# Mirroring half of a band's pixels, and shortening and reordering its reads, in a convolution and involution kernel

## The chip, the cores and the metric

The kernel runs on one core of a Trainium2 chip. The metric is the device time of one execution in microseconds (us); lower is better. Engines are named as in the profile: PE is the matrix engine (PEld its weight loads), DVE is VectorE, ACT is ScalarE, POOL is GpSimd and SP is SyncE. SP and POOL issue the transfers (DMAs); SP through the hardware queue, q1 in the profile, and POOL through the software queue, q0.

## The reference, cut to what matters

Two layers work on `x` of shape 32 x 256 x 32 x 32 (images, channels, rows, columns). Each normalizes its input in groups of eight channels (`_gn`) and adds its result to `x`.

```
# layer 0: 3x3 convolution, 256 to 256 channels, inputs and result quantized to a 10-bit mantissa
x = x + conv3x3(gn(x), weight) + bias
# layer 1: an involution; every pixel has a 7x7 kernel of its own for each of 16 groups of 16 channels
y   = relu(bn(einsum('oc,bchw->bohw', w1, gn(x))))               # 256 to 64 channels
w   = einsum('oc,bchw->bohw', w2, y) + b2                        # 16 groups x 49 taps for each pixel
out[b,g,c,h,w] = sum over k of w[b,g,k,h,w] * patches[b,g,c,k,h,w]   # 7x7 patches of gn(x), padded by 3
x = x + out
```

## The kernel before, in words

The images go through one after the other, in a software pipeline written out by hand (`manual_schedule`): the main loop counts slots n, 16 for each image, and in every slot each piece of work is issued for the image and the part that are due. Within one engine, instructions run in exactly that order; the transfers of a queue are issued in that order too.

**The front of an image** (`front`, a generator that advances one stage in each slot) computes sums for the first normalization (line 213, ACT), the quantized input `xq` (272, ACT), the 3x3 convolution `pc` (326, PE), clips it on DVE (340) and adds it to the image (342). It then normalizes again into `xn` (272), multiplies by w1 into `py` (374, PE), applies the ReLU into `y` (381, ACT) and transposes `xn` by PE (389) into `pixels` (393, ACT), in which a pixel is a partition and channels lie along the free axis.

**The pixels of an image** are cut into K = 4 bands of TR = 8 rows, and each band into two SIDES of JC = 16 columns, so that one side of one band has 8 x 16 = 128 pixels, one for each partition. Partition 16r + j holds row r and column j of the side: column j of the image on the left, column 16 + j on the right.

**The kernels of the involution** come from `weights` (404, PE, into `pw`). `evict` (428, DVE) adds the bias and writes them into a ring `w_sb` with 32 rows of the image. `scatter` (469) sends them from there to a scratch `wd` in device memory, by 28 DMAs for each image, all issued by SP. In `wd` each pixel has a record of WPIX = 1128 numbers (4512 B): seven slots of WB = 160 numbers (640 B), one for each of the seven columns that it contributes to, and 8 numbers of padding. Columns outside of the image have a place as well (S = 38 columns in all).

**A band** is a matrix that holds, for each of the 128 pixels of a side (the contraction), what it contributes to each of the 22 columns around that side. The buffer has 128 partitions, two sides and 22 slots and the padding (3528 numbers) for each side, and there are NBAND = 3 of them, zeroed once. `load_bands` (482) fills one by 16 DMAs, one for each column j of the side. Each takes 8 partitions (`j::16`), for both sides the whole record of 1128 numbers, and places it at slot j, since pixel j reaches slots j to j + 6. What it reads from `wd`, and who issues it:

```
j = i // 2 + i % 2 * JC // 2                          # 0, 8, 1, 9, 2, 10, ...
ap=[[ROW - V, TR], [JC * WPIX, SIDES], [1, WPIX]]
queue = nc.sync if i % SHARE == SHARE - 1 else nc.gpsimd
```

So SP issues columns 11 and 15 and POOL the other 14. `sums` (507, PE) multiplies `pixels` by 19 of the 22 slots of the band into `acc`: on the left slots 3 to 21, on the right 0 to 18, which are the columns inside the image. A first matmul of a band waits until all its 16 DMAs have landed. `add_windows` (523, DVE) adds `acc` to the image, and `store` (528, SP) writes it out; SP also loads the images (105).

In the order of the loop, weights run 18 slots ahead of the sums of their image, the scatter of a band comes one and two slots after the last weights that it needs, and the reads of band k are issued 9 slots ahead of its sums. POOL's instruction stream consists of almost nothing but these reads. Every read on POOL waits for the landing of POOL's eighth read before it, since there are eight semaphores to go round. The first read of a band also waits for the band's scatters and for the sums that used the buffer before. A scatter waits for the reads that last used its rows of `wd`.

Of the kernel before, what the change touches and what calls it, by code (L numbers as in the profile page):

```python
# [10 lines left out]
AF = mybir.ActivationFunctionType  # L11
# [3 lines left out]
B, C, H, W = 32, 256, 32, 32  # L15
# [5 lines left out]
K1, PAD1 = 7, 3  # L21
# [18 lines left out]
TR = RG * XR  # L40
SIDES = 2
JC = W // SIDES
# [3 lines left out]
WINC = JC + K1 - 1  # L46
# [5 lines left out]
V = 2  # L52
A = G // V
WB = G * WIN
PAD = V * (TR - XR)
WPIX = K1 * WB + PAD
# [6 lines left out]
ROW = S * WPIX  # L63
WR = 4
NBAND = 3
SHARE = 8
NPIX = 6
RING = 32
SCRATCH = 4096
# [8 lines left out]
def tile_quant_conv_then_involution(  # L78
# [10 lines left out]
    nc = tc.nc  # L89
# [50 lines left out]
    y_sb = [const.tile([P, N // 2], F32, name=f"y_{i}") for i in range(2)]  # L140
# [9 lines left out]
    wd = dram.tile([H, S, WPIX], F32, name="wd")  # L150
# [22 lines left out]
    bn_scale = const.tile([P, 1], F32, name="bn_scale")  # L173
    nc.vector.tensor_mul(bn_scale, bn[:, 0:1], bn_r)
    bn_shift = const.tile([P, 1], F32, name="bn_shift")
# [4 lines left out]
    for col, cols, at, n in (  # L180
# [4 lines left out]
        to = bass.AP(  # L185
            tensor=wd.tensor,
            offset=wd.offset + col * WPIX + at,
            ap=[[ROW, H], [WPIX, cols], [1, n]],
        )
# [83 lines left out]

    LATER = 1

    CONV = (9, 0, 9, 0)

    def front(b):
# [4 lines left out]
        def stages(n):  # L283
            for _ in range(n):
                yield

        gn = GroupNorm(b, 0)
# [18 lines left out]
        gn = GroupNorm(b, 1)  # L306
        gn.begin(N // NT)
        units = [(nt, mh) for nt in range(N // NT) for mh in range(CH)]
        for s in range(4 * len(units) + 2):
            u, i = divmod(s, 4)  # L310
            if u < len(units):
# [4 lines left out]
                elif i == 0:  # L316
                    pc = ps_c.tile([P, NT], F32, tag="pc", name="pc")
                for n in range(sum(CONV[:i]), sum(CONV[: i + 1])):


                    k = n if n < K0 * K0 else CH * K0 * K0 - 1 - n
                    kh, k = n // (K0 * K0), (k + K0 * K0 // 2) % (K0 * K0)
# [11 lines left out]
            u, i = divmod(s - 3, 4)  # L334
# [25 lines left out]
        for h in range(CH):  # L360
            yield
            to = xn[:, h].rearrange("p (k d r j) -> p d k r j", d=SIDES, r=TR, j=JC)
            at = xt[:, h].rearrange("p (k r d j) -> p d k r j", d=SIDES, r=TR, j=JC)
            gn.apply(h, [(to[:, d], at[:, d]) for d in range(SIDES)])
        yield from stages(2)

        py = ps_m.tile([P, NT], F32, tag="m", name="py")
        for r0 in range(0, H, WR):
            cols = slice(r0 // 2 * W, (r0 + WR) // 2 * W)
            for kh in range(CH):  # L370
                px = xn[:, kh].rearrange("p (k d r j) -> p k r d j", d=SIDES, r=TR, j=JC)[:, r0 // TR]
                for i in range(2):
                    r = r0 % TR + 2 * i
# [4 lines left out]
                        start=kh == 0,  # L378
                        stop=kh == CH - 1,
                    )  # L380
        nc.scalar.activation(y_sb[b % 2], py, AF.Relu, bias=bn_shift, scale=bn_scale)
        yield from stages(5)

        for m in range(0, M, 2):
# [7 lines left out]
            to = pixels[(b * M + m) // 2 % NPIX].rearrange("p i a (v c) -> p (i a) v c", c=GC)  # L392
# [78 lines left out]
    def load_bands(b, k):  # L471

        band = bands[(b * K + k) % NBAND]
        for i in range(JC):
            j = i // 2 + i % 2 * JC // 2
            src = bass.AP(
                tensor=wd.tensor,
                offset=wd.offset + k * TR * ROW + (j + PAD1) * WPIX,
                ap=[[ROW - V, TR], [JC * WPIX, SIDES], [1, WPIX]],
            )  # L480
            queue = nc.sync if i % SHARE == SHARE - 1 else nc.gpsimd
            queue.dma_start(band[j::JC, :, j * WB : j * WB + WPIX], src)  # L482

    def windows(b, m):

# [48 lines left out]
    def due(n, lag):  # L534

        b, i = divmod(n - lag, per)
        return (b, i) if 0 <= b < B else (None, None)

    with tc.manual_schedule():
        fronts = {}  # L540
        for n in range(FRONT, B * per + 2):
            b, i = due(n, FRONT)
            if i == 0:
                fronts[b] = front(b)
# [10 lines left out]
            b, i = due(n, 0)  # L555
            if b is not None and i % 2 == 0:
                sums(b, i // 2)
            b, i = due(n, 1)
# [6 lines left out]
            b, i = due(n, 2)  # L565
            if b is not None and i == 2 * (M - 1 - SIDES):
                store(b, 0)
            b, i = due(n, -LEAD)
# [3 lines left out]
            for part in range(2):  # L572
                b, i = due(n, -LEAD + 1 + part)
# [4 lines left out]
            b, i = due(n, LOAD)  # L578
# [3 lines left out]
            b, i = due(n, 3 - 4 * NBAND)  # L582
            if b is not None and i % 4 == 0:
                load_bands(b, i // 4)
# [38 lines left out]
```

## Time and profile before

| | |
|---|---|
| Time, median of 3 runs | 1371.49 us (1369.76 to 1373.4) |
| The profiled execution: its time, and its span | 1367.45 us, 1365.7 us |
| PE, busy | 1262.2 us (92%) |
| POOL, busy (all but 34 us issuing band reads) | 1012.0 us (74%) |
| DVE, ACT, busy | 819.5 us (60%), 725.7 us (53%) |
| Bytes moved by DMA | 369.95 MB, mean 271 GB/s |
| Band reads on POOL | 1792 of 70.5 KB, 548 ns each to issue, 4.8 us to land |
| Band reads on SP | 256 of 70.5 KB |
| Scatters on SP | 896 of 160 KB |

The profile shows one execution. An engine's busy time is the union of its instructions; the line number names the source line. A queue's share is the time that its packets took, as a part of the span of all 16 DMA engines. A line of waits names the engine that idled, what it was about to do, and what it waited for, then the total in us, how often, and the longest. "issue" stands where the profile shows nothing that was waited for.

### The profile page before, as it was taken

Reading aid. Unit: us, or ns where it says so; the run is one execution under the profiler, and the core shown is the slowest. Engines: PE = TensorE matmul, PEld = TensorE weight load, DVE = VectorE, ACT = ScalarE, POOL = GpSimd, SP = SyncE. Lnnn points to the kernel's source line nnn. Section 1 sums busy time; section 2 is a strip of 40 time slices with the busy share of each in tenths; the row PEclk is TensorE's granted clock in tenths of the full one; section 3 lists DMA queues with packets and bytes.
Section 4 is the critical chain, followed back from the end, with each engine's and each line's share of the span. In section 5 each row is a group of like instructions: output and inputs, shape, how many; then the busy total and the mean of one; then the engine's idle time right before and its main releaser. Section 6 shows DMA issues by size and latency. Waiting matters only on the chain.

```text
span 1365.7 us, 69351 instructions
## 1 busy us (share of the span) xinstructions
PE 1262.2 (92%) x29440; PEld 808.8 (59%) x29440; DVE 819.5 (60%) x2539; ACT 725.7 (53%) x1699; POOL 1012.0 (74%) x1818
## 2 busy tenths in 40 slices
PE   4999999999999999999999999999999998999675
PEld 2456556666566656665665666656666665666553
DVE  3466566566666656665756666666666565666542
ACT  6765656455555546565545565545656554653300
POOL 9067777777777777777777877777777777777786
PEclk9999999999999999999999999999999999999987
DMA  6199999999999999999999999999999999999996
GB/s 224 25 245 286 271 279 287 287 281 278 287 287 285 285 296 276 289 280 270 288 287 283 276 272 280 292 293 288 278 293 276 262 286 290 267 291 274 273 272 194
DMA packets 364834, 369.95 MB, mean 271 GB/s; under 512 B 77104, under 2 KB 306800, under 8 KB 364272
## 3 DMA queue, kind: packets, MB, share of 16 engines
q1 hardware_dynamic: 278512, 235.93, 57.9%
q0 software_dynamic: 86016, 129.60, 34.3%
q8 instruction: 234, 3.83, 1.2%
q14 instruction: 72, 0.59, 0.1%
HBM read 184.46 MB, written 180.76 MB: 267 GB/s over the span
## 4 chain that ended last, share of the span: by engine, by line
PE 67%; DMA 19%; issue 4%; POOL 4%; ACT 3%; DVE 2%; SPq 1%; POOLq 0%; DVEq 0%; ACTq 0%
PE pc L326 27%; PE acc L507 21%; DMA band<-wd 14%; PE pw L404 12%; DMA wd<-w_sb 5%; POOL band L482 4%; PE py L374 3%; PE pt L389 3%; ACT junk L213 1%; DVE w_sb L428 1%; SPq L469 1%; ACT xn L272 0%; DMA x<-in_x 0%; SPq L482 0%; ACT xq L272 0%
## 5 line engine op out<-in xcount | busy, mean ns | idle before, releaser
L482 POOL DMA_DIRECT2D band<-wd x1792 | 978.0, 548 | 342.9 <-DMA band<-wd 224.0
L428 DVE TENSOR_TENSOR w_sb<-pw,late_sb 128x224 f32<-128x224 f32 (+7 forms) x1280 | 331.0, 324 | 437.7 <-PE pw L404 437.6
L326 PE MATMUL pc<-xq,wq 128*128 128x496 f16 (+3 forms) x2304 | 536.0, 379 | 24.7 <-ACT xq L272 18.6
L507 PE MATMUL acc<-band,pixels 64*32 64x190 f32 (+1 forms) x16384 | 429.7, 331 | 52.0 <-DMA band<-wd 34.8
L326 PEld LDWEIGHTS <-wq 128*128 128x128 f16 x2304 | 206.5, 98 | 319.0 <-issue 106.4
L507 PEld LDWEIGHTS acc<-band,pixels 64*32 64x32 f32 x16384 | 303.2, 107 | 142.3 <-issue 94.9
L404 PE MATMUL pw<-late_sb,y 64*32 64x224 f32 (+1 forms) x8192 | 288.0, 331 | 18.7 <-issue 17.8
L523 DVE TENSOR_TENSOR x<-acc,x 128x380 f32<-128x380 f32 (+1 forms) x512 | 262.7, 513 | 31.6 <-PE acc L507 22.7
L404 PEld LDWEIGHTS pw<-late_sb,y 64*32 64x32 f32 x8192 | 186.2, 106 | 46.7 <-issue 31.9
L393 ACT COPY pixels<-pt 128x512 f32<-128x512 f32 x128 | 73.7, 576 | 241.9 <-PE pt L389 241.9
L213 ACT ACTIVATE junk<-x 128x512 f16<-128x512 f32 (+1 forms) x192 | 146.3, 762 | 14.4 <-DVE x L342 11.9
L213 ACT ACTIVATE junk<-x,mean 128x1024 f16<-128x1024 f32 x128 | 147.1, 1149 | 4.3
L244 ACT ACTIVATE s<-back,eps 128x2 f32<-128x2 f32 x64 | 18.9, 296 | 199.1 <-DVE back L229 199.0
L340 DVE TENSOR_SCALAR q<-pc 128x512 f16<-128x512 f32 x128 | 87.3, 682 | 17.1 <-PE pc L326 17.1
L272 ACT ACTIVATE xn<-x,off,rstd 128x512 f32<-128x512 f32 x128 | 96.2, 800 | 0.0
L342 DVE SCALAR_TENSOR_TENSOR x<-q,early_sb,x 128x512 f32<-128x512 f16 x128 | 94.8, 740 | 0.3
L389 PEld LDWEIGHTS pt<-ident,xn 128*128 128x128 f32 x512 | 63.8, 142 | 26.5 <-issue 3.6
L389 PE MATMUL pt<-ident,xn 128*128 128x128 f32 x512 | 77.7, 275 | 0.1
L272 ACT ACTIVATE xq<-x,off,rstd 128x1024 f16<-128x1024 f32 x64 | 75.8, 1227 | 0.2 <-PE pc L326 0.2
L374 PEld LDWEIGHTS py<-xn,early_sb 128*64 128x64 f32 x2048 | 62.6, 138 | 17.0 <-ACT mean L234 8.1
L374 PE MATMUL py<-xn,early_sb 128*64 128x64 f32 x2048 | 67.5, 224 | 3.1 <-ACT xn L272 2.2
L234 ACT ACTIVATE mean<-back 128x2 f32<-128x2 f32 x64 | 12.5, 196 | 101.4 <-DVE back L229 101.4
(40 smaller groups left out, 372.6 us busy)
## 6 DMA issues: line engine op xcount, KB each, us to landing
wd<-w_sb SPq DMA_DIRECT2D x896, 160.0 KB
band<-wd POOLq DMA_DIRECT2D x1792, 70.5 KB, 4.8
x<-in_x SPq DMA_DIRECT2D x64, 512.0 KB
out<-x SPq DMA_DIRECT2D x64, 512.0 KB
band<-wd SPq DMA_DIRECT2D x256, 70.5 KB
band<-in_w SPq DMA_DIRECT2D x2, 1152.0 KB
late_sb<-in_late SPq DMA_DIRECT2D x1, 616.0 KB
wd<-band SPq DMA_DIRECT2D x2, 180.0 KB
```

Of the source, the lines that this page charges most:

```text
L213: nc.scalar.activation(junk[:, n0:n1], src[:, h, n0:n1], func, bias=bias, accum_out=self.sums[:, i : i + 1])
L272: nc.scalar.activation(dst, src, AF.Identity, bias=self.off[:, one], scale=self.rstd[:, one])
L326: nc.tensor.matmul(pc.rearrange("p (r c) -> p r c", c=W)[:, r0 - nt * RT : r1 - nt * RT, c0:c1], wq[:, kh, k, mh * P : (mh + 1) * P], xq[: ...
L340: nc.vector.tensor_scalar(q, pc, F16_MAX, -F16_MAX, ALU.min, ALU.max)
L342: nc.vector.scalar_tensor_tensor(xt[:, mh, cols], q, bias_sb[:, mh : mh + 1], xt[:, mh, cols], ALU.add, ALU.add)
L374: nc.tensor.matmul(py[i * CR : (i + 1) * CR, cols], w1_sb[:, kh, :], px[:, r : r + 2], start=kh == 0, stop=kh == CH - 1,)
L389: nc.tensor.transpose(pt[:, i, h * P : (h + 1) * P], xn[:, h, (m + i) * P : (m + i + 1) * P], ident)
L404: nc.tensor.matmul(pws[i][t * TW : (t + 1) * TW, : dj.stop - dj.start, r], y_sb[b % 2][half, (r0 // 2 + r) * W : (r0 // 2 + r + 1) * W], w ...
L428: nc.vector.tensor_tensor(to, of[:, :, d0:d1], bias[:, :, d0:d1], ALU.add)
L482: queue.dma_start(band[j::JC, :, j * WB : j * WB + WPIX], src)
L507: nc.tensor.matmul(at[t * TW : (t + 1) * TW, h, :, f - top : l - top], px[p, a, v * GC : v * GC + TW], of[:, :, a, f - top : l - top, v], ...
L523: nc.vector.tensor_tensor(x_at, of, x_at, ALU.add)
```

## The change

The right side of each band is mirrored in the partitions: partition 16r + j now holds column 31 - j of the image on the right, and still column j on the left. `xn` is written in that order (the source is read backwards along the columns), so `pixels` follow; `y`, which has to keep the columns' natural order, is undone by a second ReLU instruction for the right side, that reads `py` backwards.

With this, the pixels of one DMA lie equally far from the two edges of the image. The slots of columns outside of the image are left out of the read: `cut` of the seven slots, 3 for j = 0, 2 for j = 1 and 1 for j = 2, on both sides. The reads of j = 0 and 1, which are the two shortest, are issued by SP (`BY_SYNC`), the other 14 by POOL. The columns are taken in another order (`ORDER`), one from each quarter of the 16 in turn. For j = 15 the two columns (15 and 16) are neighbours in `wd` and in the band, and the read becomes one run of 2256 numbers in each of 8 partitions. The number of DMAs and their places in the loop stay.

```diff
-SHARE = 8
+BY_SYNC = (0, 1)
+ORDER = (0, 4, 8, 12, 2, 5, 9, 13, 3, 1, 6, 10, 14, 7, 11, 15)
...
+    def backwards(at):
+
+        step, n = at.ap[-1]
+        return bass.AP(tensor=at.tensor, offset=at.offset + step * (n - 1), ap=[*at.ap[:-1], [-step, n]])
...
-            gn.apply(h, [(to[:, d], at[:, d]) for d in range(SIDES)])
+            gn.apply(h, [(to[:, 0], at[:, 0]), (to[:, 1], backwards(at[:, 1]))])
...
-        nc.scalar.activation(y_sb[b % 2], py, AF.Relu, bias=bn_shift, scale=bn_scale)
+        to = y_sb[b % 2].rearrange("p (r d j) -> p d r j", d=SIDES, j=JC)
+        of = py.rearrange("p (r d j) -> p d r j", d=SIDES, j=JC)
+        for d in range(SIDES):
+            at = of[:, d]
+            nc.scalar.activation(to[:, d], backwards(at) if d else at, AF.Relu, bias=bn_shift, scale=bn_scale)
...
-        for i in range(JC):
-            j = i // 2 + i % 2 * JC // 2
+        side = WINC * WB + PAD
+        for i, j in enumerate(ORDER):
+            cut = max(0, PAD1 - j)
+            n = (K1 - cut) * WB + PAD
             src = bass.AP(
                 tensor=wd.tensor,
-                offset=wd.offset + k * TR * ROW + (j + PAD1) * WPIX,
-                ap=[[ROW - V, TR], [JC * WPIX, SIDES], [1, WPIX]],
+                offset=wd.offset + k * TR * ROW + (j + PAD1) * WPIX + cut * WB,
+                ap=[[ROW - V, TR], [(W - 1 - 2 * j) * WPIX - cut * WB, SIDES], [1, n]],
             )
-            queue = nc.sync if i % SHARE == SHARE - 1 else nc.gpsimd
-            queue.dma_start(band[j::JC, :, j * WB : j * WB + WPIX], src)
+            to = band[j::JC]
+            to = bass.AP(
+                tensor=to.tensor,
+                offset=to.offset + (j + cut) * WB,
+                ap=[to.ap[0], [side + (JC - 1 - 2 * j - cut) * WB, SIDES], [1, n]],
+            )
+            queue = nc.sync if j in BY_SYNC else nc.gpsimd
+            queue.dma_start(to, src)
```

## The prediction

> **What bounds the kernel now.** I read the page first: busy times, then the DMA queues.
>
> ```profile
> span 1365.7 us, 69351 instructions
> ...
> PE 1262.2 (92%) x29440; PEld 808.8 (59%) x29440; DVE 819.5 (60%) x2539; ACT 725.7 (53%) x1699; POOL 1012.0 (74%) x1818
> ...
> DMA  6199999999999999999999999999999999999996
> ...
> q1 hardware_dynamic: 278512, 235.93, 57.9%
> q0 software_dynamic: 86016, 129.60, 34.3%
> q8 instruction: 234, 3.83, 1.2%
> ```
>
> Two resources look full: PE (92%), and the DMA engines, whose packets fill 57.9 + 34.3 + 1.3 = 93.5% of sixteen engines' span. VectorE and ScalarE have over a third of the span free. To separate the two I cut the trace where py's matmuls start, once per image. From 49.9 to 1283.3 us there are 31 intervals, mean 39.8 us, shortest 38.3 us. Stage windows (start and end, then the length, busy time by engine, granted clock, DMA share, GB/s):
>
> ```profile
> 642.60:682.30 39.70, 38.91 (x921) 25.03 (x920) 25.31 (x80) 22.55 (x54) 30.10 (x57) 1.00 1.00 285
> 723.30:764.50 41.20, 39.21 (x921) 24.95 (x920) 25.26 (x80) 22.56 (x54) 30.62 (x57) 1.00 0.97 278
> 87.00:1283.00 1196.00, 1147.66 (x27274) 738.29 (x27272) 748.11 (x2326) 660.28 (x1548) 904.64 (x1658) 1.00 0.98 282
> 1283.00:1366.00 83.00, 49.95 (x1534) 38.84 (x1520) 31.90 (x90) 3.12 (x5) 61.11 (x112) 0.82 0.84 244
> ```
>
> A slow image has the same PE work and more PE idle. In the steady stretch PE idles 1196.0 - 1147.7 = 48.3 us: 1.6 us per image is all that faster transfers can return there. In the tail it idles 33 us of 83. What ends the idle time, from the waits (total, times, longest):
>
> ```profile
> POOL band L482 <- DMA band<-wd: 224.0, 285, 2.8
> POOL band L482 <- DMA wd<-w_sb: 55.6, 28, 37.1
> PE acc L507 <- DMA band<-wd: 34.8, 17, 5.1
> PE pw L404 <- issue: 17.8, 17, 1.8
> PE acc L507 <- issue: 15.2, 19, 2.2
> POOL band L482 <- PE acc L507: 0.5, 1, 0.5
> ```
>
> POOL waits for a band buffer to be freed by PE once in the whole run; it waits 285 times for its own earlier transfers, because the order of its instructions makes each wait for the one eight before it. POOL is thus busy or held by DMA for 1355 us. Its last issue for a band comes 7.1 us on average before PE's first use, and landing takes 4.8 us: a margin near 2 us. So PE and the transfers run at almost the same pace, PE could go slightly faster, and late transfers cause part of its pauses. By place, the steady 48.3 us are 25.1 us ahead of acc (band late) and 23.3 us inside pw and conv, mostly with no releaser.
>
> The tail's chain names the transfers:
>
> ```profile
> by line: DMA band<-wd 39.1%; POOL band L482 21.2%; PE acc L507 15.0%; issue 6.7%; PE pw L404 5.1%; DMA wd<-w_sb 3.2%; DVE w_sb L428 2.3%; DVE x L523 1.0%; PE pt L389 1.0%; SPq L469 0.8%; POOLq L482 0.2%
> ```
>
> [...] a 4512 B row on q0 has a median of 182 ns (24.8 GB/s), a mean of 242, and a tenth over 404. [...] instructions come in 16 KiB blocks over a DMA queue. q8 has 234 such packets, mean 1083 ns; PE's pauses without releaser may be these, unproven.
>
> **The change, part by part.**
>
> *Shorter reads.* Columns 0, 1, 2 lose 3, 2, 1 slots of 640 B; with the right half mirrored, the same transfer loses them on columns 31, 30, 29. Eight rows, two sides: 16 x 6 x 640 = 61,440 B per band of 1,155,072, so 5.3% of the band reads and 7.9 MB of 370 (2.1%). Priced by bytes: 61,440 / 4512 = 13.6 rows x 242 ns / 16 engines = 0.21 us per band, 0.82 us per image as a mean over the engines (0.62 at the median row).
>
> *Who reads them.* SP's two reads shrink from 2 x 72,192 to 16 x (2592 + 3232) = 93,184 B. [...] POOL's column 2 saves 9.1 rows x 242 / 16 = 0.14. [...] POOL still issues 14 reads per band at 548 ns and SP two: the comparison of the two programs' orders shows the same counts, the same lanes to wait for, and SP's two still side by side behind the same scatters. No wait is added.
>
> *By quarters.* [...] The stretch to play for is 242 - 182 = 60 ns on 56 rows per engine and image = 3.4 us. [...] I bound it by a quarter of the stretch either way, +-0.84 us per image, and take zero[...].
>
> *Column 15* merges into 8 rows of 9024 B, where column 16 lies beside it. Nearest row: q1's 9216 B packets take 347 ns, against 2 x 182. Four per image, gain 0.07 us or none; POOL's issue could be cheaper than 548 ns, or dearer if it goes by bytes. I take the same.
>
> *ScalarE.* y becomes two instructions of 256 elements: 622 ns for 512 and 1042 for 1024 give 0.82 ns per element, so 768 becomes about 1116, +0.35 us per image. Reading xn backwards has no row; between free and double its element time, up to +0.84 us per image. pw reads y two slots of the loop (near 5 us) later, py comes two stages after xn; ScalarE is free 47%. Without that cover it would be 1.2 x 32 = 38 us. I take zero.
>
> *Sum.* [...] Of the 25.1 us ahead of acc I take two thirds (17 us): on average the relief covers these 0.8 us per image, but they come in bursts of up to 3.9 us; of the 23.3 us elsewhere a quarter (6 us). In the tail, 114 POOL reads go at 0.62 us each (71 us; 62 at bare issue): 3.7% of 71 is 2.6, and 2 us from starting ahead, so 5. Together 28 us: 1367.5 - 28 = 1339.5 for the profiled execution, which is 4 under the median; on the median's footing **1343.5 us**.
>
> **The rivals.** *No change:* PE is the real bound and its pauses are fetch and evictions; for it, PE's 96% in the steady stretch; against it, 34.8 us of waits on bands and POOL's never waiting for PE. Time 1371.
>
> *Larger gain:* all idle on the steady stretch goes and the tail falls to bare issue: 48 + 9 = 57, so 1315. Against it: DMA is not the only cause.
>
> *Slower:* [...] The relief is 1.47 us over 56 rows = 26 ns a row: from a mean row of 268 ns on, transfers are slower than now. [...] about +60 us: 1430; half of that excess gives about 1390. [...]
>
> *Not what it says:* that the slots are still read elsewhere. The changed program's reads are 8x2x648, 808 and 968, so this has no weight.
>
> **The numbers.** Likeliest, 1343.5, with the larger gain beside it: 0.75. No change: 0.12 (within 0.3%, about what a measurement of this kernel can tell from none). Slower: 0.13. The range reaches from near the larger gain's end to just above no change: 1318 to 1376.
>
> **What would show it.** q0 and q1 move 362 MB together with the rest; q1's share falls by more than q0's; the mean 4512 B row stays near 242 ns; intervals between py's starts come to 39.0 us; PE's waits on bands halve. ScalarE gains 32 instructions and no PE wait on y. Wrong if the row's mean passes 268 ns, if PE's idle stays at 48 us while DMA share drops, or if new waits of pw on y appear.

## The result, and the profile after

The changed kernel takes 1351.88 us (median of 20 runs, 1344.72 to 1365.11), the kernel before 1372.43 us (20 runs, 1361.98 to 1386.47). The ratio is 0.9852, with a 95% interval of 0.9831 to 0.9872: 20 us or 1.5% faster. A single run of either kernel can lie 10 us off its median. The profiled execution of the changed kernel took 1362.92 us and is one of its slowest, that of before took 1367.45 us and is one of its faster ones. So I read a second profile of the same kernel beside it, which took 1339.36 us (experiment e11).

The pages' lines on busy times, transfers and queues; first the changed kernel:

```profile
span 1361.1 us, 69383 instructions
...
PE 1264.5 (93%) x29440; PEld 808.0 (59%) x29440; DVE 819.7 (60%) x2539; ACT 733.2 (54%) x1731; POOL 1014.4 (75%) x1818
...
q1 hardware_dynamic: 278512, 229.38, 56.2%
q0 software_dynamic: 81920, 128.28, 33.4%
```

and the same kernel again (e11):

```profile
span 1337.6 us, 69383 instructions
...
PE 1249.6 (93%) x29440; PEld 801.8 (60%) x29440; DVE 820.7 (61%) x2539; ACT 733.2 (55%) x1731; POOL 1014.4 (76%) x1818
```

The bytes are the 7.9 MB fewer that were worked out (6.55 on q1, 1.32 on q0), ScalarE has its 32 instructions more, and the shares of both queues are down. PE's entry differs: the same 29,440 matmuls are "busy" for 1264.5 us in one execution and 1249.6 us in the other. The mean granted clock was 0.980 in the first and 0.990 in the second; busy time times clock gives 1239 and 1238, so here the difference goes with the clock.

By stage, in e11: up to the start of the last py, and after it (start and end, length, busy time by engine, clock, DMA share, GB/s).

```profile
87.00:1255.60 1168.60, 1138.71 (x27278) 734.45 (x27275) 748.91 (x2329) 667.80 (x1580) 909.59 (x1663) 1.00 0.96 283
1255.60:1337.60 82.00, 47.07 (x1526) 36.03 (x1520) 31.90 (x90) 3.36 (x6) 58.65 (x108) 0.84 0.80 235
```

Cut in the same places, the kernel before:

```profile
87.00:1283.30 1196.30, 1147.96 (x27277) 738.31 (x27274) 748.11 (x2326) 660.28 (x1548) 904.88 (x1659) 1.00 0.98 282
1283.30:1365.70 82.40, 49.65 (x1526) 38.82 (x1520) 31.90 (x90) 3.12 (x5) 60.87 (x112) 0.82 0.84 244
```

and the first profile of the changed kernel, cut within 0.3 us of the start of its last py:

```profile
87.00:1277.00 1190.00, 1148.45 (x27276) 739.20 (x27275) 749.15 (x2328) 667.31 (x1579) 909.78 (x1664) 0.99 0.95 277
1277.00:1361.00 84.00, 51.62 (x1535) 37.33 (x1520) 31.90 (x90) 3.73 (x7) 58.14 (x107) 0.79 0.79 233
```

In both the gain lies in the steady stretch, and the tail is as long as it was. Between the kernel before and e11 the stretch shrinks by 1196.3 - 1168.6 = 27.7 us, in the slower profile by some 6 us; the medians, 20 us apart, lie between. PE's idle time there falls from 48.3 to 29.9 us in e11 and to 41.6 us in the other. Between starts of py there are now 38.9 us on average (39.6 in the slower profile), against 39.8.

The waits of the changed kernel (its first profile; totals, times, longest):

```profile
POOL band L500 <- DMA band<-wd: 186.8, 238, 3.6
POOL band L500 <- DMA wd<-w_sb: 86.8, 44, 37.3
PE pw L414 <- issue: 23.7, 21, 2.6
PE acc L525 <- DMA band<-wd: 18.2, 11, 5.3
PE acc L525 <- issue: 14.1, 16, 2.4
```

POOL waits less for its own reads (224.0 before), and PE for bands about half as long here and 29% less in e11 (34.8 before; 24.6 in e11). POOL instead meets scatters that have not landed (55.6 before). PE's pauses inside pw without a releaser are no fewer here (17.8 before; 13.6 in e11).

### The profile page after: what moved, and what is told of

Its sections match the earlier page's. It is cut to its first block, busy times and chain, and to the rows that moved or that the text cites. A ratio compares the mean times of both kernels' runs of the same rounds, so it can differ in the third digit from the quotient of the medians.

```text
span 1361.1 us, 69383 instructions
## 1 busy us (share of the span) xinstructions
PE 1264.5 (93%) x29440; PEld 808.0 (59%) x29440; DVE 819.7 (60%) x2539; ACT 733.2 (54%) x1731; POOL 1014.4 (75%) x1818
## 4 chain that ended last, share of the span: by engine, by line
PE 72%; DMA 15%; issue 4%; POOL 3%; ACT 3%; DVE 2%; SPq 0%; POOLq 0%; DVEq 0%; ACTq 0%
PE pc L332 30%; PE acc L525 23%; PE pw L414 13%; DMA band<-wd 10%; PE py L380 4%; DMA wd<-w_sb 4%; PE pt L399 3%; POOL band L500 3%; ACT junk L214 1%; DVE w_sb L438 1%; DMA band<-in_w 1%; DVE x L541 0%; ACT xn L273 0%; DMA out<-x 0%; ACT xq L273 0%
## 5 line engine op out<-in xcount | busy, mean ns | idle before, releaser
L332 PE MATMUL pc<-xq,wq 128*128 128x496 f16 (+3 forms) x2304 | 540.1, 381 | 23.1 <-ACT xq L273 18.5
L414 PE MATMUL pw<-late_sb,y 64*32 64x224 f32 (+1 forms) x8192 | 286.2, 329 | 24.1 <-issue 23.7
L541 DVE TENSOR_TENSOR x<-acc,x 128x380 f32<-128x380 f32 (+1 forms) x512 | 262.5, 513 | 35.3 <-PE acc L525 26.4
## 6 DMA issues: line engine op xcount, KB each, us to landing
band<-wd POOLq DMA_DIRECT2D x1664, 70.5 KB, 4.6
band<-wd SPq DMA_DIRECT2D x128, 40.5 KB
```

Of the source, the lines that this page charges most:

```text
L332: nc.tensor.matmul(pc.rearrange("p (r c) -> p r c", c=W)[:, r0 - nt * RT : r1 - nt * RT, c0:c1], wq[:, kh, k, mh * P : (mh + 1) * P], xq[: ...
L414: nc.tensor.matmul(pws[i][t * TW : (t + 1) * TW, : dj.stop - dj.start, r], y_sb[b % 2][half, (r0 // 2 + r) * W : (r0 // 2 + r + 1) * W], w ...
L541: nc.vector.tensor_tensor(x_at, of, x_at, ALU.add)
```

## The experiments

All ratios are to the kernel before, run beside them; intervals are 95%. "Row" is the mean time of a 4512 B packet on POOL's queue and "store" that of a 640 B packet of the scatters, both from the trace's packet records between 87 and 1270 us. Before they are 242.0 and 35.7 ns; changed 239.7 and 35.5; changed again 234.2 and 35.4. The row's mean thus differs by 5.5 ns between two executions of one kernel, and smaller differences say nothing. A "quarter" is four neighbouring columns out of the 16 of a side (0 to 3, 4 to 7 and so on), which the expectations call a group.

**e1: the mirror alone.**

```diff
-BY_SYNC = (0, 1)
-ORDER = (0, 4, 8, 12, 2, 5, 9, 13, 3, 1, 6, 10, 14, 7, 11, 15)
+BY_SYNC = (11, 15)
+ORDER = (0, 8, 1, 9, 2, 10, 3, 11, 4, 12, 5, 13, 6, 14, 7, 15)
...
-            cut = max(0, PAD1 - j)
+            cut = 0
```

> The right half is mirrored, with everything that this needs (xn read backwards, y in two instructions, column 15 as one run), but all reads are whole records, in the old order of columns, with SP on columns 11 and 15. Theory 'bytes and queues': no bytes are saved, so the time is that of before, ratio 0.997 to 1.003. Rival 'the mirror itself counts': if the later y or the backwards reads held up PE, or the merged column 15 relieved POOL, the ratio would leave that band: up to 1.03 for the 38 us of ScalarE, or down to 0.995.

Measured: 1.0003 (0.9985 to 1.0022). The mirror is free, backwards reads and the split y included. From the changed kernel's answers on the groups by form and on y as a tile:

```profile
L273 ACT ACTIVATE xn<-x,off,rstd 128x512 f32<-128x512 f32 x128 | 96.2, 800 | 0.0
L391 ACT ACTIVATE y<-py,bn_shift,bn_scale 128x256 f32<-128x256 f32 x64 | 32.3, 554 | 13.1 <-PE py L380 13.0
...
  PEld pw L414: 0.7, 1
  PE pw L414: 0.2, 1
```

xn takes the 800 ns that it took before, so reading backwards cost nothing here. y takes 2 x 554 ns where it took 768, and in the whole run PE waited for it 0.2 us.

**e2: shorter reads, old order, SP on whole columns.** As e1, but with `cut` as in the changed kernel.

> Mirror and shorter reads; old order of columns and SP still on the whole columns 11 and 15, so POOL reads the three short ones. Theory of the prediction: the bytes count by themselves, 0.82 us per image on all 16 engines alike, so about half of the change's gain: ratio 0.990 to 0.994. Rival 'who reads decides': SP's queue[...] is what is late; then this gives nothing, 0.998 to 1.002. Rival 'order decides': also 0.998 to 1.002.

Measured: 0.9920 (0.9891 to 0.9950); row 240.7 ns. The theory's band came true: the bytes alone bring about 11 us.

**e3: the changed kernel with the old order.** As the changed kernel, with `ORDER` as in e1, so SP reads the two shortest.

> The changed kernel with the old order of columns (0, 8, 1, 9, ...); mirror, shorter reads and SP on columns 0 and 1 stay. Theory of the prediction: the order is worth nothing, so this is as fast as the changed kernel, ratio 0.985 (0.982 to 0.988), and the mean 4512 B row on POOL's queue stays at 240 to 243 ns. Rival 'the quarters bring the gain': ratio above 0.990, and the row's mean above that of the changed kernel (240 ns) by 5 ns or more.

Measured: 0.9931 (0.9905 to 0.9956); row 241.3 ns. The prediction's theory missed. Its rival had the ratio, but its second sign, a row 5 ns above the changed kernel's 240, did not come. e3 is no faster than e2: which of the reads SP has is worth nothing that these runs can tell. One more thing differs between the two: with columns 0 and 1 gone from POOL, columns 8 and 9 of one quarter follow each other there. An estimate from e10 below, where seven such pairs in each band cost 1.3 to 1.7%, puts one pair at about 0.2%, less than the gain that SP's shorter reads were to bring. What is missing to 0.9852 must come from the order, the only edit.

**e4: the order alone, in the kernel before.**

```diff
+ORDER = (4, 8, 12, 2, 5, 9, 13, 11, 3, 0, 6, 10, 14, 7, 1, 15)
...
-        for i in range(JC):
-            j = i // 2 + i % 2 * JC // 2
+        for i, j in enumerate(ORDER):
```

> The kernel before with nothing changed but the order of the columns: POOL's go through the quarters in turn (4, 8, 12, 2, 5, 9, 13, 3, 0, 6, 10, 14, 7, 1), SP keeps 11 and 15. Theory of the prediction: nothing, 0.997 to 1.003. Rival 'the quarters bring the gain': 0.985 to 0.993. [...]

Measured: 0.9948 (0.9930 to 0.9966); row 237.3 ns. The order counts by itself, about 7 us, between what the prediction's theory and its rival had asked for. With e2 it gives 0.9920 x 0.9948 = 0.9869, within the interval of the changed kernel: bytes and order account for the gain, and nothing else is needed.

**e5: columns in natural order.**

```diff
-ORDER = (0, 4, 8, 12, 2, 5, 9, 13, 3, 1, 6, 10, 14, 7, 11, 15)
+ORDER = (0, 1, 2, 3, 4, 5, 6, 7, 8, 9, 10, 11, 12, 13, 14, 15)
```

> The changed kernel with the columns in natural order, 0 to 15, so that successive reads go to partitions of the same group [...]. [...] this is the worst order of all: the mean 4512 B row rises by 10 ns or more over the 241 ns of the old order, and the time is above that of the old order with the same shorter reads: ratio above 0.996. Rival 'the order acts through something else, or e3's and e4's difference was chance': ratio 0.990 to 0.995, row 239 to 242 ns.

Measured: 1.0525 (1.0491 to 1.0560), 1438.24 us: the same bytes as e3 in another order, and 6% slower. The row's mean is 259.6 ns, and the stores, which the order does not touch, go from 35.8 to 39.1 ns. Its steady stretch and its waits:

```profile
87.00:1347.50 1260.50, 1164.17 (x27280) 749.62 (x27277) 750.03 (x2331) 670.70 (x1582) 912.78 (x1663) 0.98 0.99 262
```

```profile
POOL band L500 <- DMA band<-wd: 257.9, 330, 3.5
...
PE acc L525 <- DMA band<-wd: 55.2, 30, 5.6
```

PE idles 96.3 us in this stretch, against 41.8 in e3. Its busy time is 19 us longer, at a lower granted clock (0.984 against 0.999); the idle time is the larger part of the loss.

**e9 and e10: successive reads in different quarters, or in pairs of one quarter.** The changed kernel, with

```diff
+ORDER = (0, 2, 8, 4, 12, 9, 5, 13, 3, 1, 6, 10, 11, 14, 15, 7)    # e9
+ORDER = (0, 4, 5, 8, 9, 12, 13, 2, 3, 1, 6, 7, 10, 11, 14, 15)    # e10
```

> The changed kernel with another order: POOL's reads are paired so that two successive ones never lie in the same group of four columns, and the reads that stand first in a pair go through all four groups, as do those that stand second (groups 0 2, 1 3, 2 1, 3 0, 1 2, 2 3, 3 1). Theory [...]: as fast as the changed kernel or faster, 0.980 to 0.986. Rival [...]: 0.985 to 0.993.

> The changed kernel with the order of POOL's reads in pairs of the same group, each pair in another group than the last (1 1 2 2 3 3 0 0 1 1 2 2 3 3). Theory [...]: slow again, ratio 1.01 to 1.05, with a mean 4512 B row of 245 to 260 ns. Rival 'it was slow because the reads stay in one group for four in a row': 0.985 to 0.995.

Measured: e9 0.9890 (0.9856 to 0.9924), row 235.3, store 36.2 ns; e10 0.9984 (0.9962 to 1.0006), row 244.2, store 36.8 ns. e9 lies in the band of its rival and only touches that of its theory; it is 0.7% slower than the changed kernel beside it (e11). It is no clean test, since only the reads within a pair lie in different quarters: columns 10 and 11, and 14 and 15, still follow each other in one quarter, from one pair to the next. e10 lies just below the band of its first theory, that pairs in one quarter are enough to slow it, and above that of its rival: pairs of successive reads in one quarter cost 1.3% or more against the changed kernel, and staying in a quarter for four reads on top of it costs another 5% (e5). That changing the quarter often helps by itself is seen in e4: in the kernel before no read on POOL follows one of its own quarter, in e4 one in each band does, and e4 still gains 0.5%. Why e9 does not reach the changed kernel stays open.

One rival was not tested. Columns that follow each other in e5, e10 and the two places of e9 are not only of one quarter but also neighbours, whose records lie side by side in `wd`. No order was made of pairs of one quarter that are not neighbours, or of neighbours from different quarters. So the runs show that the order counts, and not whether it acts through the partitions of the band or through the addresses in device memory.

**e11: the changed kernel once more**, beside e9 and e10, with no edit.

> The changed kernel once more, on the same chip as the two orders beside it: ratio 0.983 to 0.988 by every theory.

Measured: 0.9820 (0.9785 to 0.9855), 1343.13 us: just below the band expected, its interval overlapping that of the first measurement. The 0.9869 worked out at e4 lies above this interval by 0.0014, less than the uncertainty of e2. e9 and e10 are best compared with this one, which ran beside them.

**e6: much shorter reads.** The changed kernel, but every read takes four slots only; the rest of the band keeps old values, so a part of the work is left out. POOL's queue moves 42% fewer bytes, all queues together 15%.

```diff
-            n = (K1 - cut) * WB + PAD
+            n = (K1 - PAD1) * WB + PAD
```

> The changed kernel with every band read cut to 648 numbers, so that on the columns 1 to 15 up to three of the seven slots are not read and the band keeps old values there (that part of the computation is left out). Same number of reads, issues and waits; 42% less of the bytes on the band queue. It shows what relief of the DMA engines can bring at most. Prediction's 'larger gain': all of PE's idle time but its start goes, 1315 us, ratio 0.955 to 0.965. Rival 'half of the steady idle time has another cause': 23 us inside pw and conv stay, ratio 0.97 to 0.98. Rival 'POOL's issue bounds': at 14 x 548 ns per band it cannot, ratio unchanged at 0.985 would show it.

Measured: 0.9599 (0.9567 to 0.9631), 1309.61 us, in the band of the prediction's larger gain. Its stages, cut in the same way:

```profile
87.00:1229.20 1142.20, 1131.21 (x27278) 733.66 (x27276) 747.78 (x2327) 666.25 (x1579) 921.58 (x1664) 1.00 0.86 244
1229.20:1306.90 77.70, 50.14 (x1524) 38.56 (x1520) 31.90 (x90) 4.16 (x8) 57.98 (x105) 0.81 0.70 206
```

With the DMA share at 0.86 PE idles 11.0 us in the steady stretch (48.3 before), and its busy time is 16.8 us shorter than before. The clock does not explain that: e3 has the same mean clock in this stretch (0.999) and 1145.1 us of busy time, 14 us more. Starts of py come 38.0 us apart on average, the least of any kernel here. PE's pauses inside pw without a releaser are fewer too, 6.9 us where they were 17.8:

```profile
PE pw L414 <- issue: 6.9, 10, 1.4
```

How far those pauses depend on the load of the DMA engines is not shown: the changed kernel has 23.7 and 13.6 us in its two profiles, e8 below 23.1 with less full engines, e5 13.2 with the fullest. That they are fetches of instructions (before, q8 has 234 packets of 16,384 B, mean 1083 ns) was not shown either.

**e7 and e8: three reads on SP, or none.**

```diff
-BY_SYNC = (0, 1)
+BY_SYNC = (0, 1, 2)    # e7
+BY_SYNC = ()           # e8
```

> The changed kernel with column 2 given to SP as well: POOL issues 13 reads per band instead of 14, SP three. Theory 'POOL's chain of reads (eight in flight) is the late one': shorter by one fourteenth, ratio 0.975 to 0.983. Theory of the prediction[...]: slower than the changed kernel, 0.988 to 0.995. Rival 'who reads is worth nothing' (as e2 and e3 suggest): 0.983 to 0.988.

> The changed kernel with all 16 reads on POOL and none on SP. POOL issues 16 x 548 ns = 8.8 us per band of about 10. Theory [...] faster than the changed kernel, 0.978 to 0.984. Theory 'POOL's chain is the late one': two more reads in it, slower, 0.99 to 1.01. Rival 'who reads is worth nothing': 0.983 to 0.988.

Measured: e7 1.0023 (1.0003 to 1.0044), e8 1.0941 (1.0903 to 1.0979). For e8 the waits, and the queues' part of the page:

```profile
POOL band L500 <- DMA band<-wd: 187.4, 224, 2.5
...
PE acc L525 <- DMA band<-wd: 119.0, 59, 6.6
```

```profile
q1 hardware_dynamic: 272368, 217.44, 49.3%
q0 software_dynamic: 90112, 140.24, 33.0%
```

PE waits for bands more than three times as long as before (34.8) although the DMA engines are less full (82% against 92% in these two queues), so it is not fuller engines that delay them. What got longer is POOL's chain of reads: issuing takes 64 x 551 ns = 35.3 us of each image's 43.2, and the last read of a band is issued 5.1 us on average before its first use, where it was 7.0 before. With 4.4 us to land the margin is nearly gone. Faster landing could still help, since POOL also waits 187.4 us for its own reads. With three on SP the chain is shorter, but:

```profile
POOL band L500 <- DMA wd<-w_sb: 160.8, 70, 37.6
POOL band L500 <- DMA band<-wd: 151.5, 195, 3.2
```

POOL now waits for scatters (55.6 us before) more than for its own reads: what POOL gains is lost on SP's queue, which issues the scatters too. SP has less slack: its waits for new weights fall to 77.5 us, from 176.3 in the changed kernel. The row is no longer than in the changed kernel (237.3 ns). All three theories missed e7. All three bands missed e8 as well; only the theory of POOL's chain had the direction. The prediction's theory for e7 and the first one for e8 rest on the author's estimate that SP's reads load some DMA engines more than others, which is not shown. Whether in e7 it is SP's time to issue or the packets on its queue that makes the scatters late was not separated.

## Why the prediction was right, and where its steps failed

**Direction and mechanism hold.** Late transfers were part of the bound: fewer bytes brought 0.8% with nothing else changed (e2 against e1), and much shorter reads 4.0% (e6). The point forecast was 1343.5 us, 28 us of gain; 20 us came. That it came so near is partly luck: a term that brought nothing and a term put at zero that brought a third to half of the gain stand against each other.

**Readings of the profile.** Three were off. Of the 31 intervals between starts of py, three are shorter than 38.3 us (27.8, 35.3 and 37.8). The 1355 us in which POOL is "busy or held by DMA" include 48 us in which it waits for nothing that the profile shows; without these and other small waits it is 1292. And "25.1 us ahead of acc (band late)" is right as a sum, but not in its cause. The steady stretch before, and then the tail:

```profile
PE acc L507 <- issue: 12.7, 17, 2.2
PE acc L507 <- DMA band<-wd: 10.4, 8, 3.9
```

```profile
PE acc L507 <- DMA band<-wd: 24.4, 9, 5.1
```

Only 10.4 of the 25.1 us are put down to bands, and 24.4 of the 34.8 us of waits on bands lie in the tail. So the forecast of 17 us ahead of acc was too high: PE's idle time there fell to 16.8 us in e11 and to 17.4 in the slower profile, by 8 us. Of the 23 us elsewhere 10 went in e11 and none in the other, where 6 were forecast.

**"Who reads them" was mis-sized.** The step gave 1.47 us of relief per image (3.7% of 39.8) on half of the sixteen DMA engines: 16 rows of 235 ns on each of eight are 3.76 us, which SP's shorter reads make 2.43, so 1.33, and 0.14 for POOL's column 2. That SP's rows keep to eight engines, and that these are the busier ones, was the author's estimate. In the packet records of before at most eight of SP's 4512 B rows are under way at once, but for 0.1 of the 328 us in which there are any; the records name no engine, so that it is always the same eight, and that they are busier, is not shown. e2 and e3 differ in who has the short reads (and in the one pair of columns named there) and are 0.9920 and 0.9931: no gain. The likely reason is seen in the trace of before: SP's last read for a band is issued 16 us on average before its first use and POOL's last one 7, so SP's are not the late ones. What remains of the term is the mean relief of 0.82 us per image, and 11 us of gain for it.

**"By quarters: zero" was wrong.** The order is worth 0.5% by itself (e4) and about 0.8% on top of the shorter reads (0.9852 / 0.9931). The bound of +-0.84 us per image held. The zero was the author's estimate. The trace names neither the engine nor the partitions of a packet, so what the order acts through is not shown.

**The slower rival came true in another order, and its threshold was wrong.** e5 costs 5% to 6%. The rival put the turning point at a mean row of 268 ns; e5 is 5% slower at 259.6. Its 26 ns of slack came from the 1.47 us that were mis-sized; with 0.82 us it is 15 ns, and the turning point 257. And it counted band rows only: in e5 the stores take 3.4 ns more than before, and at 448 for each engine and image (28 scatters x 256 / 16) that is 1.5 us, more than the 56 rows x 18 ns = 1.0 us. What lengthens the stores was not separated; in e6, with fewer bytes to move, they take 37.2 ns. Its 1390 does not follow from its own figures: half of its 60 us gives about 1400. Why e5's rows take longer is not shown; the order is its only edit against e3, whose mean row is 241.3 ns.

**"1.6 us of PE idle per image is all that can be returned" was too low, by a little.** e6 takes 54.1 us out of the steady stretch, of which 37.3 were idle time and 16.8 stood in the profile as busy. The prediction's larger gain was about reached (0.9599, and 1315 / 1372 = 0.958), but of other parts than the 48 us of idle time and 9 us of tail that it had added up.

**The tail: 5 us taken, nothing seen.** It lasts 82.4 us before, 82.0 in e11, 83.8 in the slower profile. Its chain in e11:

```profile
by line: DMA band<-wd 32.9%; POOL band L500 21.8%; PE acc L525 11.1%; issue 10.7%; DMA wd<-w_sb 5.4%; PE pw L414 5.3%; DVE w_sb L438 4.3%; DVE x L541 2.3%; PE pt L399 0.7%; POOLq L637 0.7%; SPq L479 0.6%; POOLq L500 0.2%
```

Reads and POOL's issuing still lead it, with the same number of reads. Even with 42% fewer bytes on POOL's queue it is still 77.7 us long (e6).

**Edits costed at nothing.** Mirror, backwards reads, split y and merged column 15 together: confirmed (e1). POOL's issue at 548 ns whatever the size: confirmed, 549 after the change. Of the signs named beforehand, the bytes, ScalarE's 32 instructions and the row near 242 ns came (239.7 and 234.2), and PE waited for y 0.2 us. q1's share fell by more than q0's in one profile (1.7 against 0.9 points) and by as much in the other, waits on bands halved in one, and the interval of 39.0 us lies between the two profiles' 38.9 and 39.6.

No version that does the whole work beats the changed kernel: e9, the only other order made to be good, is 0.9890.

## What to carry to other kernels

When a queue of many small transfers feeds an engine, price the bytes, the length of the issuing chain and the order of the transfers each by itself; here the order of sixteen reads was worth nearly as much as leaving out 5% of their bytes, and a bad order cost 6%. Look at both ends before moving reads between queues: here one read more on SP cost 1.7% and two more on POOL 11% against the changed kernel, so the balance of 14 and 2 was tight on both sides. And do not take an engine's idle time in the profile for an upper bound of what relief can return: in e6 PE's idle time in the steady stretch fell by 37.3 us and its busy time by 16.8 us as well. Why the busy time fell was not shown.

## What was not expected of the hardware

- Reading backwards along 16-element runs cost ScalarE nothing here: xn takes 800 ns in both kernels; the two instructions of y, one of which reads `py` backwards, take 544 to 567 ns.
- The order of the band reads alone slowed another queue's packets: SP's stores of 640 B went from 35.8 to 39.1 ns (e3 to e5).
- POOL's issue takes 548 to 557 ns for a read of 16 rows, from 40.5 KB to 70.5 KB (before and e6), so that in this kernel the number of reads and not their size set what issuing cost.
- PE's busy time for the same 29,440 matmuls ran from 1245.8 us (e6) to 1291.5 us (e8). Most of this goes with the granted clock, 0.986 and 0.956 on average. Busy time times clock still runs from 1229 (e6) and 1234 (e8), with DMA shares of 0.86 and 0.87 in the steady stretch, over 1239 and 1238 for the changed kernel (0.95 and 0.96) to 1244 before (0.98): in these five executions it is higher where the DMA share is higher, to within 1 us.
